# Layer 0's tail in chunks of 8, 4 and 10 tiles, split early tables, and other places for the gather buffers

## The chip, the cores and the metric

The kernel runs on one core of a Trainium2 chip. A core has TensorE (PE), VectorE (DVE), ScalarE (ACT), GpSimd (POOL) and SyncE (SP), each with its own instruction queue, which it works off in order; between queues, semaphores order the work. The metric is the device time of one execution in microseconds (us).

## The reference, cut to what matters

Four graph layers run over N = 2708 nodes with D = 128 features. `adj` is a 2708 x 2708 matrix with about 0.3% of its entries non-zero, each row scaled to sum one.

```python
# layer 0: hyperbolic layer on h = relu(layernorm(x))
h = h_add(h_mul(h, embed), embed_bias)
neigh = exp_map_zero(adj @ log_map_zero(h))
x = x + h_add(h_mul(concat(h0, neigh), layer), layer_bias)   # h0: the layer's input
# layer 1: messages over edges, on h = relu(layernorm(x))
s = h @ msg_w[:, :D].T
d = h @ msg_w[:, D:].T
messages = gelu(s[:, None, :] + d[None, :, :] + msg_b)
aggregated = einsum('ijd,ij->id', messages, adj)
new = concat(h, aggregated) @ upd_w.T + upd_b
x = x + layernorm(gelu(new) + h)
# layer 2: x += relu(adj @ (h @ W));  layer 3: x += h @ W_self + (adj @ h / deg) @ W_neigh
```

In the hyperbolic layer, `exp_map_zero` takes a norm and a tanh, `log_map_zero` a norm and an arctanh (by logarithms), and `h_add` some dot products and a division for every row. Layer 1 needs, for each node i, the rows d[j] of its neighbours j: only those are gathered.

## The kernel before, in words

The nodes lie in T = 22 tiles of 128 rows (the last has 20), and six blocks: five of 4 tiles and one of 2. The dense products with `adj` of layers 0, 2 and 3 are made with a mask (non-zero or not) per block of columns and three bf16 parts of the other operand (`add_product`, 66 matmuls for a block of layer 0). The value by which the mask is scaled is one number per row, `val`, which POOL gathers from `adj`.

From the mask the kernel also finds, for each node, the columns of its neighbours. PE packs the mask into words (`words_in`, `pack`: 22 matmuls and some for the transpose `wp`), VectorE finds up to 24 of them by repeated maxima (`find_words`) and turns them into indices (`find_columns`, `lay_out`). The first 6 neighbours of a node have places of their own: 2 of them (EARLY) are gathered ahead of the loop into `early`, 4 (HEAD − EARLY) in the loop into `g`. All further ones go to the tail: 3 chunks of 128 edges a tile, gathered into `gt` by indices `tail_c`, which `mark_edges` and `pack_edges` prepare. A neighbour beyond the reach of the early table has the index of a row of large negative numbers (`none`) in its early place, and is put in the tail.

Layer 0's tail is what follows each block's product: `neighbours` (norm, tanh, product with half of `layer`, sums of squares), then in `update` `log_factor` and `moebius` (small instructions on one number per row, Ln and Tanh on ScalarE), the new x with its statistics, and `normal_form` (layer 1's layernorm as scale and offset). Then, for each block, `normal_tiles` (relu on ScalarE, transpose hTpm on PE, copy) and the product d on PE, a copy of d into `v` on ScalarE, and a write of d from SP's queue to tables in memory. Before the change all of this runs in two chunks: blocks 0, 1 and 2 (12 tiles), and the late ones 3, 4 and 5 (10 tiles). One table `d_early` holds the d of the first 12 tiles; `d_hbm` holds all. In the middle of the kernel the order is:

```python
        product(2, sums)
        neighbours([0, 1, 2], sums)
        ...
        last = add_product(4, acc, range(split_at))
        formed = update([0, 1, 2], nc.scalar.copy, last)
        ...
        find_columns(slice(groups[3].stop, T))
        gather_early(range(first_half))
        ...
        last = neighbours(late, sums)
```

`find_columns` ends with the gathers of `val` (one per tile) on POOL's queue. `gather_early` puts one gather per tile and early slot on that queue. So POOL's queue holds, one behind the other: val of the last six tiles, 24 early gathers of tiles 0 to 11, 18 of the late tiles, and then those of the loop.

The loop runs over the tiles: for each, `messages` issues 4 gathers into `g` and up to 3 into `gt`, VectorE adds the row's own part, ScalarE takes gelu, and PE sums. Matmuls of layer 2 (`two`) fill PE between tiles. `prelude` prepares a group's own parts on PE, VectorE and ScalarE: that of group 0 runs after all six `pack_edges`, those of later groups in the loop. The gather buffers come from the pool `gath` (4 of each kind), which is opened after the pools of the first part are closed, so that its memory is that of tiles of the first part, and a gather waits until those are done with. `queue_behind` sets an order for the scheduler, which otherwise fills each engine's queue by priority.

After the last tile come the rest of layers 2 and 3.

Of the kernel before, what the change touches and what calls it, by code (L numbers as in the profile page):

```python
# [556 lines left out]
def sparse_stack(  # L557
# [169 lines left out]

    d_hbm = dram.tile([NP + 1, D], F32, name="d_hbm")
    d_early = dram.tile([first_half * P + 1, D], F32, name="d_early")
# [18 lines left out]
    def load_later():  # L748

        nc.gpsimd.dma_start(out=d_hbm[NP : NP + 1, :], in_=none)  # L750
        nc.gpsimd.dma_start(out=d_early[first_half * P :, :], in_=none)
        for w, src in (
            (msg_w, msg_wt),
            (upd_w, upd_wt),
            (w2_w, w2),
            (self_w, w_self),
            (neigh_w, w_neigh),
        ):
            nc.gpsimd.dma_start(out=w, in_=src.rearrange("(a p) o -> p a o", p=P))
        for r, src in ((msg_br, msg_b), (upd_br, upd_b), (ln_wr, ln_w), (ln_br, ln_b)):  # L760
            nc.gpsimd.dma_start(out=r, in_=src.partition_broadcast(P))
# [25 lines left out]


# [7 lines left out]
    with ExitStack() as st:  # L796

        words_p = st.enter_context(tc.tile_pool(name="words", bufs=2))
        left_p = st.enter_context(tc.tile_pool(name="left", bufs=2))
        wide = st.enter_context(tc.tile_pool(name="wide0", bufs=1))  # L800
# [9 lines left out]
        shifts = wide.tile([P, T, P], BF16, name="shifts")  # L810
        for t in range(T):
            nc.gpsimd.tensor_scalar_mul(shifts[:, t, :], ident, float(2 ** (T - 1 - t)))

        spread = r_all[:, full, tails(full) * P :]
        nc.gpsimd.memset(spread, 0.0)
        apart = wide.tile([P, HEAD, rest], F32, name="apart")
# [19 lines left out]
        place = wide.tile([P, P], I32, name="place")  # L836
# [85 lines left out]
        def normal_tiles(sl, name, copy, after=None):  # L922

            n = sl.stop - sl.start
            for t in range(sl.start, sl.stop):
                nc.scalar.activation(  # L926
                    h[:, t, :],
                    x[:, t, :],
                    AF.Relu,
                    bias=node("nb")[:, t : t + 1],  # L930
                    scale=node("rstd")[:, t : t + 1],
                )
# [24 lines left out]
        def times_bias(w, bias, out, name):  # L957
# [3 lines left out]
            wT = pair_p.tile([P, P], F32, tag="wT", name=f"wT{name}")  # L961
# [60 lines left out]
        def pack(b):  # L1022
# [4 lines left out]
            for t in range(T):  # L1027
                nc.tensor.matmul(  # L1028
                    pk[:, :w], shifts[:, t, :], mask[:, t, sl], start=(t == 0), stop=(t == T - 1)
                )  # L1030
            return pk

        def words_in(b):
# [5 lines left out]
            pk = pack(b)  # L1039
# [87 lines left out]

        def lay_out(sl):
# [5 lines left out]
            from_c = float((T - first_half + 1) * P)  # L1134
# [4 lines left out]
            nc.vector.tensor_scalar(near, first[:, :, :EARLY], from_c, None, op0=ALU.is_ge)  # L1139
            nc.vector.scalar_tensor_tensor(  # L1140
                cand[:, sl, 2, SLOTS - EARLY :],
                first[:, :, :EARLY],
                from_c,
# [7 lines left out]
                -(from_c + first_half * P),  # L1151
# [4 lines left out]
            if sl.stop < T:  # L1156
                nc.vector.tensor_scalar_add(early_c[:, sl, :], miss, float(first_half * P))
# [92 lines left out]
        def pack_edges(b, after):  # L1250

            t0, t1 = blocks[b]
            n = t1 - t0
            px = ps_one.tile([P, BANK], F32, tag="one", name=f"ex{b}")
            px = px[:, : n * NQ * 32].rearrange("p (t q c) -> p t q c", t=n, c=32)
            for k in range(n):
                t = t0 + k
                for q in range(NQ):
                    with queue_behind(after):
                        nc.tensor.matmul(  # L1260
                            px[:, k, q, : TAIL + 3],
                            r_all[:, t, q * P : (q + 1) * P],
                            edge_x[:, t, :] if q < tails(t) else short_x,
                            start=True,
                            stop=True,
                        )
            ex = small.tile([P, BLOCK, NQ, TAIL + 3], F32, tag="ex", name=f"exs{b}")
            nc.scalar.copy(ex[:, :n], px[:, :, :, : TAIL + 3])  # L1268
            m = n * NQ
            kth, past, jump = (  # L1270
                small.tile([P, BLOCK * NQ], F32, tag=name, name=f"{name}{b}")[:, :m]
                for name in ("kth", "past", "jump")
            )
            flat_ex = ex.rearrange("p t q c -> p (t q) c")[:, :m, :]
            edge = small.tile([P, BLOCK, NQ], F32, tag="edge", name=f"edge{b}")[:, :n, :]
# [3 lines left out]
                tail_r[:, t0:t1, :].rearrange("p t q -> p (t q)"), flat_ex[:, :, TAIL + 2]  # L1279
            )  # L1280

            nc.vector.tensor_sub(kth, edge, flat_ex[:, :, TAIL])
            nc.vector.tensor_tensor(past, edge, flat_ex[:, :, TAIL + 1], ALU.is_ge)
            nc.vector.tensor_sub(jump, flat_ex[:, :, TAIL], flat_ex[:, :, TAIL + 1])
# [4 lines left out]
            sel = small.tile([P, BLOCK * NQ, TAIL], F32, tag="sel", name=f"sel{b}")[:, :m, :]  # L1289
# [6 lines left out]
            nc.vector.tensor_mul(sel, sel, flat_ex[:, :, :TAIL])  # L1296
            cf = small.tile([P, BLOCK * NQ], F32, tag="cf", name=f"cf{b}")[:, :m]
            nc.vector.tensor_reduce(cf, sel, AX.X, ALU.add)
            nc.vector.tensor_scalar_add(
                tail_c[:, t0:t1, :].rearrange("p t q -> p (t q)"), cf, MID  # L1300
            )
            if t1 == T:
                q = (n - 1) * NQ + tails(full)
                nc.vector.tensor_mul(sel[:, q, :HEAD], is_place, flat_ex[:, q, :HEAD])
                nc.vector.tensor_reduce(cf[:, q : q + 1], sel[:, q, :HEAD], AX.X, ALU.add)
                nc.vector.tensor_scalar_add(
                    tail_c[:, full, tails(full) : tails(full) + 1], cf[:, q : q + 1], MID
                )
# [47 lines left out]
        def neighbours(bs, sums):  # L1356
# [3 lines left out]
            nc.vector.tensor_mul(n_sq, sums[0][:, : sl.stop - sl.start], val[:, sl])  # L1360
            nc.vector.tensor_mul(n_sq, n_sq, val[:, sl])
            _, r, n = norm(n_sq, sl, "k")
            nc.scalar.activation(th, n, AF.Tanh)
# [6 lines left out]
            for t0 in range(sl.start, sl.stop, 3):  # L1370
                g = slice(t0, min(t0 + 3, sl.stop))
                ps = tiles_times(g, yT, layer_w[:, 1, :], f"ne{t0}")
# [19 lines left out]
        def update(bs, copy, after):  # L1392
# [21 lines left out]
            formed = normal_form(sl)  # L1414
            for b in bs:
                g = groups[b]
                n = g.stop - g.start
                normal_tiles(g, f"m{b}", copy, after)
# [3 lines left out]
                for table, end in ((d_early, first_half), (d_hbm, T)):  # L1422
# [7 lines left out]
            return formed  # L1430
# [88 lines left out]
        def gather_early(ts):  # L1519
            for t in ts:  # L1520
                n = rows(t)
                for k in range(EARLY):
                    nc.gpsimd.indirect_dma_start(  # L1523
                        out=early_d[t // EACH][:n, t % EACH, k, :],
                        out_offset=None,
                        in_=d_early,
                        in_offset=bass.IndirectOffsetOnAxis(ap=early_c[:n, t, k : k + 1], axis=0),
                    )
# [3 lines left out]
        sums = sums_of([0, 1, 2])  # L1532
# [10 lines left out]
        end_product(1, acc, sums)  # L1543
        lay_out(halves[0])
        with queue_behind(scaled):
            nc.vector.tensor_scalar(
                spread[:, : HEAD * rest].rearrange("p (k r) -> p k r", r=rest), apart, 0.0, None,
                op0=ALU.is_equal, saturate=False,
# [5 lines left out]
        find_words(3, words_in(3))  # L1554
        find_columns(groups[3])
        read_block(4)
        product(2, sums)
        neighbours([0, 1, 2], sums)
        read_block(5)
        sums = sums_of(late)  # L1560
        product(3, sums)
        words = {b: words_in(b) for b in (4, 5)}
        acc = begin_product(4)
        split_at = BLOCK
        last = add_product(4, acc, range(split_at))
        formed = update([0, 1, 2], nc.scalar.copy, last)
        find_words(4, words[4], formed)
# [5 lines left out]
        add_product(4, acc, range(split_at, T), latest["times"])  # L1573
        end_product(4, acc, sums)
        find_words(5, words[5], formed)
        product(5, sums)
        find_columns(slice(groups[3].stop, T))
        gather_early(range(first_half))
# [5 lines left out]
        with queue_behind(last):  # L1584
            nc.vector.tensor_scalar_add(
                early_c[:, halves[1], :], late_c, float(first_half * P)
            )
        gather_early(range(first_half, full))
        formed = update(late, nc.vector.tensor_copy, None)
        for b in (2, *late):  # L1590
            mark_edges(b, formed)
        for b in range(nb):
            pack_edges(b, latest["times"])
# [98 lines left out]

    group_p = held.enter_context(tc.tile_pool(name="group", bufs=3))
    with ExitStack() as st_m:
        hot_p = st_m.enter_context(tc.tile_pool(name="hot", bufs=3))
        gath_p = st_m.enter_context(tc.tile_pool(name="gath", bufs=4))
        small = st_m.enter_context(tc.tile_pool(name="small1", bufs=2))
        junk_p = st_m.enter_context(tc.tile_pool(name="junk", bufs=1))

        def prelude(g):  # L1700

            sl = groups[g]
            n = sl.stop - sl.start
            for t in range(sl.start, sl.stop, 2):
                two = slice(t, min(t + 2, sl.stop))
                m = two.stop - t
                ps = ps_one.tile([P, BANK], F32, tag="one", name=f"own{t}")
                ps = ps[:, : m * 2 * D].rearrange("p (n j d) -> p n j d", j=2, d=D)
                for k in range(m):
                    nc.tensor.matmul(  # L1710
                        ps[:, k, :, :],
# [347 lines left out]
```

## Time and profile before

| | us |
|---|---|
| median of 3 runs (range) | 554.39 (553.61 to 556.01) |
| the profiled execution's own time | 553.8 |
| its span | 552.0 |
| PE busy | 420.9 (76%) |
| VectorE busy | 422.0 (76%) |
| ScalarE busy | 239.5 (43%) |
| POOL busy | 237.2 (43%) |
| mean granted TensorE clock | 0.892 |

The span is the time from the first to the last instruction that the profiler saw; some 1.8 us of the execution's time lie around it. The page cuts the span into 40 slices of 13.8 us and gives each engine's busy share in tenths; layer 0's tail is in slices 7 to 15. In the timelines a line has start, duration, engine, line of the kernel, operation, output and input, and in brackets how long the engine was idle ahead of it and what ended the wait.

### The profile page before, as it was taken

To read this page: it belongs to the slowest core of one execution; us is meant where nothing else is said; L and a number is where in the kernel's file an instruction comes from. 1 tells how busy PE (TensorE), PEld (TensorE's weight loads), DVE (VectorE), ACT (ScalarE), POOL (GpSimd) and SP (SyncE) were. 2 spreads that over 40 slices of the span, in tenths; PEclk is the share of its full clock that TensorE was granted. 3 is DMA by queue.
4 is the path that set the end of the run, shared out by engine and by line. 5 is a ranking of instruction groups with operands and counts; after the bars stand their busy time and mean duration, and the time that the engine had idled before them with its cause. 6 is when DMAs were issued, how large, how long until landed. Compare 5 with 4: busy or idle time off the path is not lost.

```text
span 552.0 us, 8233 instructions
## 1 busy us (share of the span) xinstructions
PE 420.9 (76%) x2504; PEld 266.1 (48%) x2504; DVE 422.0 (76%) x1743; ACT 239.5 (43%) x570; POOL 237.2 (43%) x268
## 2 busy tenths in 40 slices
PE   1981999999994071376786869859878999989994
PEld 1760344464753051264654656646545455445652
DVE  6877977767998989537788787986656699998742
ACT  2867966766424131324643545444644344300100
POOL 8900022220047777777777777777770000000000
PEclk9995899999997555568897999998998999999998
DMA  8893779970041132123246364672220150399111
GB/s 263 292 300 128 228 243 334 310 212 2 1 116 48 48 92 52 52 52 100 53 153 199 109 195 153 173 232 54 54 52 7 66 237 1 120 382 386 36 57 51
DMA packets 39332, 77.89 MB, mean 141 GB/s; under 512 B 5754, under 2 KB 18614, under 8 KB 37722
## 3 DMA queue, kind: packets, MB, share of 16 engines
q1 hardware_dynamic: 30270, 63.15, 33.1%
q0 software_dynamic: 7264, 13.40, 9.8%
q10 hardware_dynamic: 1744, 0.72, 0.5%
q8 instruction: 22, 0.36, 0.3%
q14 instruction: 32, 0.26, 0.1%
HBM read 73.63 MB, written 3.62 MB: 140 GB/s over the span
## 4 chain that ended last, share of the span: by engine, by line
DVE 34%; PE 32%; issue 9%; POOL 8%; ACT 8%; DMA 7%; ACTq 0%; DVEq 0%; SPq 0%
PE three L1645 8%; PE acc L1324 6%; POOL g L1727 4%; PE two L1645 3%; POOL gt L1727 3%; DVE eq L1661 3%; PE msg L1789 2%; DMA a<-in_adj_t_dram 2%; PE pk L1028 2%; DMA layer_w<-in_L_gnn_layer_dram 2%; DMA g<-d_hbm,head_c 1%; PE u L1458 1%; PE d L948 1%; PE msg L1791 1%; ACT h L1626 1%
## 5 line engine op out<-in xcount | busy, mean ns | idle before, releaser
L1645 PEld LDWEIGHTS <-parts 128*128 128x128 bf16 x792 | 74.5, 99 | 79.8 <-ACT parts L1630 4.4
L1727 POOL DMA_INDIRECT g<-d_hbm,head_c x84 | 83.3, 991 | 25.8 <-issue 20.4
L1645 PE MATMUL two<-mask,parts 128*128 128x512 fp8e4 (+1 forms) x396 | 82.0, 361 | 3.3 <-ACT parts L1630 3.1
L1324 PE MATMUL acc<-mask,parts 128*128 128x512 fp8e4 (+1 forms) x396 | 80.3, 358 | 0.4 <-DVE parts L786 0.4
L1645 PE MATMUL three<-mask,parts 128*128 128x512 fp8e4 (+1 forms) x396 | 79.0, 354 | 0.6 <-ACT parts L1630 0.5
L1727 POOL DMA_INDIRECT gt<-d_hbm,tail_c x65 | 63.1, 971 | 19.8 <-issue 15.5
L1120 POOL DMA_INDIRECT val<-in_adj_dram,ai x22 | 22.1, 1003 | 104.0 <-DVE left L1108 91.2
L1324 PEld LDWEIGHTS <-parts 128*128 128x128 bf16 x396 | 36.9, 98 | 47.1 <-ACT parts L783 7.5
L1523 POOL DMA_INDIRECT early<-d_early,early_c x42 | 43.0, 1023 | 12.8 <-issue 11.6
L1789 PE MATMUL msg<-ident,early 128*128 128x128 f32 x84 | 17.0, 333 | 39.7 <-DVE gt L1778 29.4
L999 ACT ACTIVATE mask<-a 128x2048 fp8e4<-128x2048 uint32 (+3 forms) x27 | 38.2, 1434 | 10.6 <-DMA a<-in_adj_t_dram 10.5
L1661 DVE TENSOR_SCALAR_CACHE_REDUCE eq<-row,val 128x2708 fp8e4<-128x2708 f32 (+1 forms) x13 | 39.4, 3030 | 4.4 <-DMA row<-in_adj_dram 4.3
L1028 PE MATMUL pk<-mask,shifts 128*128 128x512 fp8e4 (+1 forms) x132 | 31.3, 376 | 12.5 <-ACT mask L999 12.5
L1789 PEld LDWEIGHTS msg<-ident,early 128*128 128x128 f32 x84 | 13.2, 222 | 43.5 <-DVE gt L1778 21.9
L1661 DVE TENSOR_SCALAR_CACHE_REDUCE eq<-hT,val 128x1354 fp8e4<-128x1354 f32 x18 | 29.2, 1620 | 0.0
L1789 PE MATMUL msg<-ident,g 128*128 128x128 f32 x168 | 27.8, 318 | 0.0
L1789 PEld LDWEIGHTS msg<-ident,g 128*128 128x128 f32 x168 | 26.1, 233 | 0.3
L1775 DVE TENSOR_TENSOR g<-g,v 128x512 f32<-128x512 f32 x21 | 14.5, 692 | 15.2 <-DMA g<-d_hbm,head_c 15.2
L1710 PE MATMUL own<-pair_w,hT 128*128 128x256 f32 x44 | 15.4, 489 | 13.5 <-ACT exs L1268 9.6
L926 ACT ACTIVATE h<-x,n_nb,n_rstd 128x128 f32<-128x128 f32 x44 | 18.1, 485 | 16.6 <-DVE n_nb L920 16.6
L1791 PE MATMUL msg<-rt,gt 128*128 128x128 f32 x130 | 22.1, 317 | 0.7 <-ACT gt L1784 0.7
L936 PE MATMUL hTpm<-ident,h 128*128 128x128 f32 x22 | 5.6, 350 | 21.7 <-ACT h L926 21.7
(407 smaller groups left out, 877.1 us busy)
## 6 DMA issues: line engine op xcount, KB each, us to landing
a<-in_adj_t_dram SPq DMA_DIRECT2D x25, 1024.0 KB, 7.4
row<-in_adj_dram SPq DMA_DIRECT2D x12, 1354.0 KB, 9.3
hT<-in_adj_dram SPq DMA_DIRECT2D x18, 677.0 KB, 4.1
a<-in_adj_t_dram SPq DMA_DIRECT2D x5, 296.0 KB, 4.6
g<-d_hbm,head_c POOLq DMA_INDIRECT x84, 2.7
a<-in_adj_t_dram SPq DMA_DIRECT2D x5, 256.0 KB
d_hbm<-v SPq DMA_DIRECT2D x5, 256.0 KB, 3.7
out_dram<-x SPq DMA_DIRECT2D x5, 256.0 KB
```

The source lines that it names most:

```text
L926: nc.scalar.activation(h[:, t, :], x[:, t, :], AF.Relu, bias=node("nb")[:, t : t + 1], scale=node("rstd")[:, t : t + 1],)
L999: nc.scalar.activation(mask[:, g : g + n, sl], bits[:, :n, :w], AF.Sign, saturate=False)
L1028: nc.tensor.matmul(pk[:, :w], shifts[:, t, :], mask[:, t, sl], start=(t == 0), stop=(t == T - 1))
L1120: nc.gpsimd.indirect_dma_start(out=val[:, t : t + 1], out_offset=None, in_=flat, in_offset=bass.IndirectOffsetOnAxis(ap=ai[:, t : t + 1], ...
L1324: last = nc.tensor.matmul(acc[:, :w], parts[:, t, k, :], mask[:, t, sl], start=(t == 0 and k == 0), stop=(t == T - 1 and k == 2),)
L1523: nc.gpsimd.indirect_dma_start(out=early_d[t // EACH][:n, t % EACH, k, :], out_offset=None, in_=d_early, in_offset=bass.IndirectOffsetOnAx ...
L1645: last = nc.tensor.matmul(accs[b][:, : sl.stop - sl.start], parts[:, t, k, :], mask[:, t, sl], start=(t == 0 and k == 0), stop=(t == T - 1 ...
L1661: last = nc.vector.tensor_scalar(eq[:n, : c1 - c0], a, val[:n, t : t + 1], None, op0=ALU.is_equal, op1=ALU.add, accum_out=same[:n, t, k : ...
L1710: nc.tensor.matmul(ps[:, k, :, :], hT[:, (t + k) * P : (t + k + 1) * P], pair_w[:, 0::2, :], start=True, stop=True,)
L1727: nc.gpsimd.indirect_dma_start(out=g[:n, q, :], out_offset=None, in_=d_hbm, in_offset=bass.IndirectOffsetOnAxis(ap=table[:n, q : q + 1], a ...
L1789: nc.tensor.matmul(sums, part, ident, start=(q == 0), stop=False)
L1791: done = nc.tensor.matmul(sums, gt[:, q, :], rt[:, q, :], start=(not own_places and q == 0), stop=(q == nq - 1),)
```

## The change

Layer 0's tail is cut in three chunks: blocks 0 and 1 (8 tiles), block 2 (4 tiles), and the late blocks (10 tiles). The early table becomes two: `d_early8` with the first 8 tiles, read by early slot 0, and `d_early12` with the first 12, read by slot 1. The limits in `lay_out` become small tiles with one value per slot. The making of d leaves `update` and is a function of its own, `make_d`, whose parts get places of their own in the queues.

```diff
+    reach = [groups[1].stop, first_half]
-    d_early = dram.tile([first_half * P + 1, D], F32, name="d_early")
+    d_early = [dram.tile([n * P + 1, D], F32, name=f"d_early{n}") for n in reach]
...
-            nc.vector.tensor_scalar(near, first[:, :, :EARLY], from_c, None, op0=ALU.is_ge)
+            nc.vector.tensor_tensor(near, first[:, :, :EARLY], each(from_c, n), ALU.is_ge)
...
-        def update(bs, copy, after):
+        def update(bs):
...
-            formed = normal_form(sl)
+            return normal_form(sl)
+
+        def make_d(bs, copy, after=None, relu_after=None):
             for b in bs:
                 g = groups[b]
-                normal_tiles(g, f"m{b}", copy, after)
+                normal_tiles(g, f"m{b}", copy, after, relu_after)
                 ps = tiles_times(g, hT, msg_w[:, 1, :], f"d{b}", mirrored=True)
                 nc.scalar.copy(d, ps)
-                for table, end in ((d_early, first_half), (d_hbm, T)):
+                for table, end in ((d_early[0], reach[0]), (d_early[1], reach[1]), (d_hbm, T)):
```

The order written out by hand becomes (the middle part of it):

```diff
+        neighbours([0, 1], sums)
+        words = {3: words_in(3)}
+        read_block(4)
+        sums = sums_of([2])
+        product(2, sums)
+        times = times_layer([2])
+        acc = begin_product(3)
+        last = add_product(3, acc, range(2 * BLOCK))
+        read_block(5)
+        words.update((b, words_in(b, last)) for b in (4, 5))
+        last = add_product(3, acc, range(2 * BLOCK, 4 * BLOCK), latest["pack"])
+        formed = update([0, 1])
         lay_out(halves[0])
...
+        done = neighbours([2], sums, formed, times)
+        make_d([0, 1], nc.scalar.copy, last, latest["th"])
+        find_words(3, words[3])
         find_columns(groups[3])
...
+        gather_early(range(first_half), [0])
+        sums = sums_of(late)
+        add_product(3, acc, range(4 * BLOCK, T), last)
+        end_product(3, acc, sums)
+        acc = begin_product(4)
+        last = add_product(4, acc, range(T))
         end_product(4, acc, sums)
+        formed = update([2])
+        find_words(4, words[4], done)
+        find_words(5, words[5], done)
+        make_d([2], nc.scalar.copy, last)
         product(5, sums)
         find_columns(slice(groups[3].stop, T))
-        gather_early(range(first_half))
+        gather_early(range(first_half), [1])
...
-        gather_early(range(first_half, full))
-        formed = update(late, nc.vector.tensor_copy, None)
+        gather_early(range(first_half, full), range(EARLY))
+        formed = update(late)
+        make_d(late, nc.vector.tensor_copy)
```

On POOL's queue the 12 gathers of early slot 0 of tiles 0 to 11 now stand ahead of the six late gathers of val; behind val come the 12 of slot 1, the 18 of the late tiles and the loop. On PE's queue the packs of blocks 4 and 5 and the transposes and products hTpm0, d0, hTpm1, d1 stand inside block 3's product, hTpm2 and d2 inside block 5's. On ScalarE's queue the relus of blocks 0 and 1 stand behind the tanh of block 2's `neighbours`.

`pack_edges` takes one or two blocks at a time, and `prelude` of group 0 is issued after the first of them, with scratch memory of its own:

```diff
-        for b in range(nb):
-            pack_edges(b, latest["times"])
+        through = latest["times"]
+        packed = pack_edges([0], through)
...
+        first = prelude(0, ps_one, lambda t, m: halves_of[t // 2], packed)
+        pack_edges([1, 2], through)
+        pack_edges(late[:2], through)
+        pack_edges(late[2:], through)
...
+    gath_p = held.enter_context(tc.tile_pool(name="gath", bufs=4))
     group_p = held.enter_context(tc.tile_pool(name="group", bufs=3))
...
-        gath_p = st_m.enter_context(tc.tile_pool(name="gath", bufs=4))
```

The pool `gath` is opened ahead of `group`, and so lies over the tiles of the pools `words`, `left` and a new pool `first0` (the shift matrices of the packs and two tables of positions), all of which are used for the last time in the first part.

## The prediction

> **What bounds the kernel now.** I read the table of busy tenths first, then the costliest groups, then the timeline of POOL, and last the timelines of VectorE and ScalarE around the places where POOL stood still.
>
> ```profile
> PE   1981999999994071376786869859878999989994
> PEld 1760344464753051264654656646545455445652
> DVE  6877977767998989537788787986656699998742
> ACT  2867966766424131324643545444644344300100
> POOL 8900022220047777777777777777770000000000
> PEclk9995899999997555568897999998998999999998
> ...
> L1727 POOL DMA_INDIRECT g<-d_hbm,head_c x84 | 83.3, 991 | 25.8 <-issue 20.4
> ...
> L1727 POOL DMA_INDIRECT gt<-d_hbm,tail_c x65 | 63.1, 971 | 19.8 <-issue 15.5
> L1120 POOL DMA_INDIRECT val<-in_adj_dram,ai x22 | 22.1, 1003 | 104.0 <-DVE left L1108 91.2
> ...
> L1523 POOL DMA_INDIRECT early<-d_early,early_c x42 | 43.0, 1023 | 12.8 <-issue 11.6
> ```
>
> POOL is busy only 43% of the span, but its digit is 7 without a break from slice 12 to slice 29, with only "issue" between instructions. A stretch of 7s with no other releaser is an engine that can go no faster: one gather takes about 0.95 us and 0.30 us of issue. The timeline gives the ends of that stretch:
>
> ```profile
> 157.61 0.95 POOL L1120 DMA_INDIRECT val<-in_adj_dram,ai  x1 [38.20 <-DVE left L1108]
> ...
> 164.41 1.34 POOL L1120 DMA_INDIRECT val<-in_adj_dram,ai  x1 [0.30 <-issue]
> 166.05 0.94 POOL L1523 DMA_INDIRECT early<-d_early,early_c  x1 [0.31 <-issue]
> ...
> 222.03 1.03 POOL L1727 DMA_INDIRECT g<-d_hbm,head_c  x1 [0.53 <-ACT parts L783]
> ...
> 412.53 0.95 POOL L1727 DMA_INDIRECT gt<-d_hbm,tail_c  x1 [0.30 <-issue]
> ```
>
> From 157.61 to 413.48 POOL runs 6 + 42 + 84 + 65 = 197 gathers in 255.9 us, 1.30 us each. Before that it idles 38.2 us for column indices from VectorE. After it come 552.0 − 413.5 = 138.5 us in which PE is the dense engine. So the span is (start of POOL's last run) + 255.9 + 138.5, and what the change can move is that start, or a hole inside the run.
>
> The hole is near: the first loop gather needs all of layer 1's d in memory. On VectorE and ScalarE:
>
> ```profile
> 169.66 0.17 DVE L1360 TENSOR_TENSOR n_nsq<-nsq,val 128x10 f32<-128x10 f32 x1 [1.24 <-DMA early<-d_early,early_c]
> ...
> 192.16 0.17 DVE L920 SCALAR_TENSOR_TENSOR n_nb<-n_tn,n_rstd 128x10 f32<-128x10 f32 x1
> ```
> ```profile
> 203.54 0.37 ACT L1421 COPY v<-d 128x256 f32<-128x256 f32 x1 [1.64 <-PE d L948]
> ```
>
> The late ten tiles begin at 169.66, which is 5.25 us after the last val gather was issued at 164.41: the first wait there is for val, whatever releaser is named. The last d copy ends at 203.91, its write is issued at 203.95, and transfers of that size are over by about 206.5 in the DMA view. That is 36.8 us after 169.66. POOL itself reaches the loop at 222.03, so the late chain has 15.5 us to spare now.
>
> [...] a g gather lands 2.7 us after its issue (median), and a 256 KB d write 3.7 us. [...] every gather from a d table is charged the landing of the write, as the chain of waits does. [...] The trace shows the load at 1.28 us and the next activation 0.02 us behind it; I charge 1.28. [...] 0.17 us for 12 columns and 0.17 us for 10. A chunk cut in two pays its small instructions twice.
>
> **The change part by part.**
>
> *Chunks 8 and 4 in place of 12.* VectorE issues a second set of small instructions: some 16 in neighbours, 45 in log_factor and moebius, 15 in normal_form. A dependent one takes 0.20 us from start to start, an interleaved one 0.08. In the trace neighbours took 2.5 us up to n_rk, log and moebius 126.7 to 135.5 less a wait of 2.5, normal_form 2.6. That is 11 to 13 us more VectorE work, of which a part is interleaved with find_words. Two to three table loads more cost ScalarE 1.28 each. In exchange the first 8 tiles need no third block, and three idle spots of VectorE (2.46 at 107.06, 4.60 at 120.00, 2.48 at 129.85) can be filled.
>
> *When the first gather can start.* In the changed order POOL's long run begins with 12 gathers (tiles 0 to 11, first slot) from a table of the first 8 tiles. My hand timeline, from rows of before, on VectorE: find_words(3) from 110.8 (its wt cast now sits behind one more mask), 5.2 us, then n_t at 118.4. ScalarE has three masks (1.91 and 0.70 us) and a table load ahead of n_e: 122.8. Moebius 1.9: 124.7. x and its statistics 2 × 2.9: 130.5. normal_form 2.6: 133.1. neighbours of block 2 runs next and its tanh ends at about 136; the eight relus are queued behind that on ScalarE, with two casts and the squares, until 141.8. PE in its written order (66 matmuls of a block 14.4 us, two packs of 22) is at hTpm0 at 139.6, and at about 143 with a stall of 2.7 us that I count at nsq2, which waits for ScalarE. Then hTpm0, its copy (0.58), d0, the logarithms and n_e in between (1.28 + 0.21 each table), the second copy, d1, v copied at 150.6. The write is issued at 150.7; landing takes 3.4, between the 3.28 of one d write in the chain of waits and the median of 3.7, which gives **154.1**, against 157.61 now: 3.5 us earlier. Bounds: with no ScalarE queueing and no PE stall 147; with the same terms doubled 163.
>
> *The vals behind those 12.* The late column indices are ready at about 156, but the six val gathers now stand behind 12 others: 12 × 1.28 = 15.4 us. Their last is issued at start + 15.4 + 6.8, and the late chain begins 5.25 later, at start + 27.4 = 181.5 instead of 169.66. VectorE would be ready at about 167 and PE at 173 to 174, so both wait for val: here the stall goes. Queued behind that n_nsq on VectorE is the whole late chain, 14 mark_edges and the edge packs. The late d lands 36.8 later, at start + 64.2, or 218.3. This is the cover of the 15.5 us, now used up.
>
> *POOL's own way to the loop* has the same 48 gathers as now, 64.4 us (222.03 − 157.61). It arrives at start + 64.4 too. So both limits meet, and the first g is at about start + 64.5 = 218.6. The gain there is 222.03 − 218.6 = 3.4 us.
>
> *Buffers and packs.* Now the gather buffers lie over tiles that the packs and the prelude last use; after, over tiles done much earlier. That removes the 0.53 us ending in "ACT parts", and more importantly keeps VectorE's later end from holding POOL: the packs, now 45 instructions in place of 68, end at about 230 in the changed order. The first tail indices (about 220) are due to POOL at about 227. I cost this at nothing beyond the above; with the old placement the prelude's end would have been late next.
>
> *Tables and queues.* Two more 256 KB writes on SP, and one more row of 512 B on POOL's queue early on: SP's d writes are 2.2 us apart now, so some 0.4 us of issue each hides, except the one in front of the 8-tile table, already in 154.1. Constants per slot and the different early misses replace like with like: nothing. PE's total work stays the same.
>
> *Loop and end.* In the loop PE's last use of a tile's buffers precedes POOL's reuse by 13 to 21 us (tile 0: 237.3 against 258.05), so a shift of 3 or 4 us passes through to 409.9, and the 138.5 us after it stay.
>
> Sum: the profiled execution is 553.8 us (span 552.0). 553.8 − 3.4 = 550.4. The median of the runs shown is 554.39, 0.6 above it; I say 550.5, since the timeline is no better than that.
>
> **The rivals.** *A larger gain.* For it: PE has no natural wait before 139.6, and VectorE's idle spots hold 9.5 us. If the first gather starts at 148, everything moves until PE's 174 becomes the limit of the late chain: 174 + 36.8 = 210.8 for d, and 212.4 for POOL: about 9.6 us, 544. Against it: five ScalarE waits stand in a row before d1's copy.
>
> *Slower, by one mechanism.* The first d is now on an in-order path: ScalarE's relus behind a tanh that needs VectorE, PE's hTpm0 behind 48 matmuls of block 3 and two packs, the copies behind a table load. And the vals, which need none of that, are queued behind gathers that do. Each us that d1's write lands later costs one us in POOL's run and one in the late chain. The deciding point is a start at 157.6; at 160.4 it is 0.5% slower. A start at 163 gives 163 + 64.5 − 222.03 = 5.5 us, 559. For it: the 13 us of extra small VectorE work and three table loads are certain, the filling of the idle spots is not.
>
> *No change.* The chain ends between 154.8 and 160.4, and early gathers only swap places with vals: 551 to 556.6. That the buffers still hold POOL is not to be seen in the order of instructions; if it were so, the first g would wait for the prelude at about 225, also slower by 3 us.
>
> **How the numbers follow.** 0.5%, about what a measurement of this kernel can tell from no change, is 2.8 us. Start 3 to 6 us earlier: 0.38. Larger gain: 0.10. No change: 0.20. Slower: 0.32, because an in-order path across three engines is seldom as short as its rows. The likeliest case's own range is 548 to 551.6; the range that holds 8 in 10 goes from 544.5 to 560.
>
> **What would show it.** Right: POOL's first early gather at about 154, ahead of all late vals; n_nsq of the late tiles at about 181 with a wait of about 10 us for val; the first g at about 218.6, released by d's write or following without a gap; the last gt ending at about 410; 138.5 us after it. Wrong: a first early gather after 158, or a gap on POOL ahead of the first g of over 3 us, or gaps later in the loop, or an end that is not 138.5 us long.

## The result, and the profile after

The changed kernel takes 550.85 us (median; 548.81 to 553.86), the kernel before, on the same chips, 553.36 us (550.91 to 556.01). The ratio is 0.996, with a 95% interval of 0.9943 to 0.9977: faster by 0.4%. The forecast was 550.5 us, with a gain of 3.4 us; the gain of the medians is 2.5 us. As the next sections show, the sum came out near because two of its terms were wrong by some 4 us each, with opposite signs: that is luck. One run, of 551.61 us in the first experiment, was in a slower state of the chip: it is left out of the ratio there, and the median, 545.45, is 544.22 without it.

The page of the changed kernel, its busy tenths for POOL and its groups of gathers (line, engine, operation, output and input, count, then busy time, mean ns of one, and the idle time ahead with its main releaser):

```profile
POOL 8900022220087777777777777777770000000000
...
L1788 POOL DMA_INDIRECT g<-d_hbm,head_c x84 | 81.5, 971 | 25.6 <-issue 20.1
...
L1788 POOL DMA_INDIRECT gt<-d_hbm,tail_c x65 | 64.9, 999 | 19.8 <-issue 15.8
...
L1580 POOL DMA_INDIRECT early<-d_early,early_c x42 | 47.8, 1138 | 39.8 <-DMA d_early<-v 27.3
...
L1160 POOL DMA_INDIRECT val<-in_adj_dram,ai x22 | 21.0, 954 | 71.0 <-DVE left L1148 56.4
```

POOL's unbroken stretch begins one slice earlier (slice 11 instead of 12, counted from 0; a slice is 13.7 us). The long wait of POOL is now ended by the write of d to an early table, and a mean early gather takes 1138 ns instead of 1023. POOL's timeline shows where that comes from:

```profile
150.17 0.95 POOL L1580 DMA_INDIRECT early<-d_early,early_c  x1 [27.28 <-DMA d_early<-v]
...
157.75 0.99 POOL L1580 DMA_INDIRECT early<-d_early,early_c  x1 [0.30 <-issue]
159.05 5.90 POOL L1580 DMA_INDIRECT early<-d_early,early_c  x1 [0.30 <-issue]
165.26 0.94 POOL L1580 DMA_INDIRECT early<-d_early,early_c  x1 [0.30 <-issue]
...
176.51 0.94 POOL L1160 DMA_INDIRECT val<-in_adj_dram,ai  x1 [0.31 <-issue]
...
218.28 0.94 POOL L1788 DMA_INDIRECT g<-d_hbm,head_c  x1 [0.30 <-ACT exs L1314]
...
408.87 0.94 POOL L1788 DMA_INDIRECT gt<-d_hbm,tail_c  x1 [0.30 <-issue]
```

The run starts at 150.17, 7.44 us earlier than before. But the 48 gathers up to the first g take 68.11 us and not 64.42: one of them, at 159.05, takes 5.90 us. The last gather ends at 409.81. The span is 547.1 instead of 552.0, which adds up as −7.44 (start) + 3.69 (the 48 gathers) + 0.08 (the 149 gathers of the loop, 191.53 against 191.45) − 1.23 (what follows, 137.29 against 138.52) = −4.90. The last of these terms is not counted to the change: over the ten executions profiled here that stretch took 137.3 to 141.2 us. That it was at its shortest in this execution may also be why the execution (548.94 us) lies under its own median.

VectorE during the long gather (start, duration, line, operation):

```profile
158.45 1.13 DVE L1282 SCALAR_TENSOR_TENSOR r_all<-edge_i,n_off,before 128x384 fp8e4<-128x384 f16 x2
...
162.54 0.54 DVE L1279 TENSOR_SCALAR before<-edge_i,n_end 128x384 f16<-128x384 f16 x2
163.00 1.14 DVE L1282 SCALAR_TENSOR_TENSOR r_all<-edge_i,n_off,before 128x384 fp8e4<-128x384 f16 x2
169.09 0.17 DVE L1257 COPY n_off<-po 128x10 f32<-128x10 f32 x1 [4.95 <-PE po L1256]
...
179.63 0.17 DVE L1413 TENSOR_TENSOR n_nsq<-nsq,val 128x10 f32<-128x10 f32 x1 [9.93 <-DMA val<-in_adj_dram,ai]
```

From 157.91 to 164.14 VectorE works off the eight mark_edges of blocks 0 and 1 with no gap. The gather ends at 164.95, 0.81 us after the last of them. The late n_nsq at 179.63 waits 9.93 us for val, and the first g waits for nothing but its turn.

### The profile page after: what moved, and what is told of

Its sections match the earlier page's. It is cut to its first block, busy times and chain, and to the rows that moved or that the text cites. A ratio compares the mean times of both kernels' runs of the same rounds, so it can differ in the third digit from the quotient of the medians.

```text
span 547.1 us, 8301 instructions
## 1 busy us (share of the span) xinstructions
PE 411.4 (75%) x2504; PEld 257.6 (47%) x2504; DVE 424.8 (78%) x1805; ACT 241.8 (44%) x576; POOL 241.1 (44%) x269
## 4 chain that ended last, share of the span: by engine, by line
DVE 33%; PE 24%; POOL 12%; ACT 10%; issue 10%; DMA 10%; ACTq 0%; DVEq 0%; SPq 0%; POOLq 0%
PE three L1727 9%; POOL g L1788 5%; PE two L1727 3%; POOL gt L1788 3%; POOL early L1580 3%; DMA g<-d_hbm,head_c 3%; DMA a<-in_adj_t_dram 3%; PE msg L1850 2%; DVE eq L1743 2%; ACT mask L1034 2%; DMA layer_w<-in_L_gnn_layer_dram 2%; PE acc L1366 1%; DMA gt<-d_hbm,tail_c 1%; PE u L1516 1%; ACT h L1708 1%
## 5 line engine op out<-in xcount | busy, mean ns | idle before, releaser
L1788 POOL DMA_INDIRECT g<-d_hbm,head_c x84 | 81.5, 971 | 25.6 <-issue 20.1
L1727 PE MATMUL two<-mask,parts 128*128 128x512 fp8e4 (+1 forms) x396 | 83.3, 365 | 3.3 <-ACT parts L1712 3.1
L1788 POOL DMA_INDIRECT gt<-d_hbm,tail_c x65 | 64.9, 999 | 19.8 <-issue 15.8
L1580 POOL DMA_INDIRECT early<-d_early,early_c x42 | 47.8, 1138 | 39.8 <-DMA d_early<-v 27.3
L1160 POOL DMA_INDIRECT val<-in_adj_dram,ai x22 | 21.0, 954 | 71.0 <-DVE left L1148 56.4
L1803 PE MATMUL msg<-parts,r_all 128*128 128x128 bf16 x195 | 15.4, 228 | 22.9 <-ACT exs L1314 19.9
L1850 PE MATMUL msg<-ident,g 128*128 128x128 f32 x168 | 26.2, 305 | 0.0
L1803 PEld LDWEIGHTS <-r_all 128*128 128x128 fp8e4 x195 | 12.8, 102 | 25.9 <-issue 20.0
L1850 PEld LDWEIGHTS msg<-ident,g 128*128 128x128 f32 x168 | 24.4, 219 | 0.2
```

The lines of the kernel that those rows point to most:

```text
L1160: nc.gpsimd.indirect_dma_start(out=val[:, t : t + 1], out_offset=None, in_=flat, in_offset=bass.IndirectOffsetOnAxis(ap=ai[:, t : t + 1], ...
L1580: nc.gpsimd.indirect_dma_start(out=early_d[t // EACH][:, t % EACH, k, :], out_offset=None, in_=d_early[k], in_offset=bass.IndirectOffsetOn ...
L1727: last = nc.tensor.matmul(accs[b][:, : sl.stop - sl.start], parts[:, t, k, :], mask[:, t, sl], start=(t == 0 and k == 0), stop=(t == T - 1 ...
L1788: nc.gpsimd.indirect_dma_start(out=g[:n, q, :], out_offset=None, in_=d_hbm, in_offset=bass.IndirectOffsetOnAxis(ap=table[:n, q : q + 1], a ...
L1803: latest["source"] = nc.tensor.matmul(ps[:, q * D : (q + 1) * D], r_all[:, t, q * P : (q + 1) * P], parts[:, t, k, :], start=(k == 0), sto ...
L1850: nc.tensor.matmul(sums, part, ident, start=(q == 0), stop=False)
```

## The experiments

Two theories stood against each other. **Theory 1**: POOL's run sets the end, its start is what the change gained, and the row of marks on VectorE holds a gather of POOL's up, the one of 5.90 us, and takes half of the gain back. **Rivals**: the long gather is chance or comes from the d writes; or the late chain behind val, the chunks or the buffers set the first g.

**Marks while POOL is idle.** The marks of blocks 0 and 1 move to where POOL waits for d, behind n_t of block 2 (`latest["t"]`; the line that keeps it is left out here).

```diff
         formed = update([2])
+        for b in (0, 1):
+            mark_edges(b, latest["t"])
...
-        for b in (0, 1):
-            mark_edges(b, formed)
```

> The changed kernel, with the eight mark_edges of blocks 0 and 1 moved on VectorE's queue from behind lay_out (157.91 to 164.14 in the changed kernel's trace, while POOL issues gathers) to behind n_t of block 2 (about 143.5 to 150, while POOL waits). Theory 1 [...]: no early gather over 2.2 us before the vals, the 48 gathers from the first early one to the first g in 62 to 64 us instead of 68.1, first g at about 213.5, execution 4 to 5 us shorter than that of the changed kernel with the 5.9 us gather, so about 544 to 547. Rival (the long gather comes from the d writes or from chance on the DMA side): a gather of 3 us or more is still there or is there in some runs, time as the changed kernel's, 549 to 551. Second rival (late d is the limit just behind): POOL gains but stops ahead of the first g for the d_hbm write; first g no earlier than about 215.5.

It took 545.45 us, 0.9864 of the kernel before (0.9828 to 0.9901). POOL's timeline of this run:

```profile
148.38 1.56 POOL L1580 DMA_INDIRECT early<-d_early,early_c  x1 [27.28 <-DMA d_early<-v]
...
170.34 0.94 POOL L1160 DMA_INDIRECT val<-in_adj_dram,ai  x1 [0.30 <-issue]
...
200.21 2.07 POOL L1580 DMA_INDIRECT early<-d_early,early_c  x1 [0.30 <-issue]
...
212.19 0.94 POOL L1788 DMA_INDIRECT g<-d_hbm,head_c  x1 [0.30 <-ACT exs L1314]
```

No gather before the vals takes over 1.56 us, and the 48 gathers take 63.81 us (212.19 − 148.38), 4.3 less than in the changed kernel. That the run also starts 1.8 us earlier is no more than what its start differs by between kernels with the same order ahead of it (147.96 to 150.17). Two of the eight tiles' marks were still left over when POOL began; they ran between other instructions and held no gather. The first g still has no wait of its own. Theory 1 holds, the rival of the d writes does not: they are still there, at the same place.

**Marks twice.** The suspected cost is doubled, in time that VectorE had idle.

```diff
         for b in (0, 1):
             mark_edges(b, formed)
+        for b in (0, 1):
+            mark_edges(b, formed)
```

> The changed kernel, with the eight mark_edges of blocks 0 and 1 issued twice at their place (same values written again, VectorE's row of marks 12.4 us long instead of 6.2; VectorE was idle after it until 179.6). Theory 1 (the row of marks starves POOL): the stretched gathers inside the row add up to about 10 to 12 us instead of 5.0 over their usual length, first g about 6 us later (224), time 555 to 557. Rival (the 5.9 us gather has another cause): VectorE's idle time hides the second row, the time stays at 549 to 552.

It took 557.56 us, 1.0071 of before (1.0036 to 1.0106), 6.7 more than the changed kernel. POOL, and the last marks of the row on VectorE:

```profile
158.93 11.97 POOL L1580 DMA_INDIRECT early<-d_early,early_c  x1 [0.30 <-issue]
```
```profile
168.94 1.14 DVE L1282 SCALAR_TENSOR_TENSOR r_all<-edge_i,n_off,before 128x384 fp8e4<-128x384 f16 x2
```

One gather took 11.97 us, ending at 170.90, again 0.82 after the row's end at 170.08. The first g was at 223.95.

**Vals first.** The `gather_early` of slot 0 is issued behind `find_columns` of the late tiles.

```diff
-        gather_early(range(first_half), [0])
         ...
         find_columns(slice(groups[3].stop, T))
+        gather_early(range(first_half), [0])
```

> The changed kernel, with the six late val gathers put ahead of the twelve slot-0 early gathers on POOL's queue. The prediction's account (POOL's run is the limit, and the late chain behind val has as much room): POOL's run starts when the late column indices are ready, about 153.2 instead of 150.2; the late tiles' n_nsq moves from 179.6 to about 172, where PE ends; the end moves later by the 3 us of the start, to 552 to 554. Rival (the late chain behind val sets the first g): the first g comes earlier, and the time falls by 2 us or more, to 547 to 549.

It took 550.4 us (0.9951, 0.993 to 0.9971), like the changed kernel, and not the 552 to 554 expected. The edit did less than described: the scheduler left four of the twelve early gathers ahead of the vals, so POOL began at 149.22 and not later. But the question is answered. The late n_nsq came at 169.11, 10.5 us earlier than in the changed kernel, and the first g at 217.50, no earlier than POOL's own pace allows (68.28 us after the start, with a val gather of 5.91 us beside the marks). An earlier late chain brought nothing; in this kernel it costs nothing that the vals stand behind others.

**Gather buffers at the old place.**

```diff
-    gath_p = held.enter_context(tc.tile_pool(name="gath", bufs=4))
...
         hot_p = st_m.enter_context(tc.tile_pool(name="hot", bufs=3))
+        gath_p = st_m.enter_context(tc.tile_pool(name="gath", bufs=4))
```

> The changed kernel, with the pool gath opened where it was before the change, behind group and hot, so that the gather buffers lie over other tiles of the first part. The prediction's account (with the old place the end of the packs or of the prelude would hold the first loop gathers): POOL stands still ahead of some g or gt until VectorE's packs are done (tail_c of the last block at 241.8 in the changed kernel's trace, prelude at 221), 3 to 20 us, time 552 to 570. Rival (the place of the buffers does not matter, since POOL has no slack to lose there): no wait of POOL over 1 us ahead of g, 549 to 552.

It took 563.35 us, 1.019 of before (1.0143 to 1.0236). The first g on POOL:

```profile
231.44 0.94 POOL L1788 DMA_INDIRECT g<-d_hbm,head_c  x1 [15.96 <-DVE tail_c L1348]
```

POOL stood still for 15.96 us until tail_c, the end of the last pack on VectorE (230.61). With the packs and the prelude in their new order, the new place of the buffers is what keeps VectorE out of POOL's way.

**One early table.** Both slots read the table of 12 tiles; all early gathers stand behind val, as before (the line that names the tables is left out here).

```diff
-    reach = [groups[1].stop, first_half]
+    reach = [first_half, first_half]
...
-        gather_early(range(first_half), [0])
...
+        gather_early(range(first_half), [0])
         gather_early(range(first_half), [1])
```

> The changed kernel with the early tables not split: both slots read a table of the first 12 tiles, and all 24 early gathers of tiles 0 to 11 stand behind the six late vals on POOL's queue, as before the change; chunks, PE and ScalarE order, packs and buffers stay as changed. The prediction's account (the gain is POOL's earlier start, which only the 8-tile table gives): POOL issues val from about 153 to 160, then waits for block 2's d, which lands at about 170 (its write is issued at 166.4 in the changed kernel's trace), then needs 42 gathers of 1.27 us, so the first g is at about 223 to 224, that is 5 to 6 us later than in the changed kernel; 555 to 557. Rival (the gain comes from the chunks themselves or from the buffers): first g at about 218 and 549 to 552.

It took 556.9 us, 1.0078 of before (1.0053 to 1.0103). POOL's timeline:

```profile
151.89 1.10 POOL L1160 DMA_INDIRECT val<-in_adj_dram,ai  x1 [30.19 <-DVE left L1148]
...
158.57 1.34 POOL L1160 DMA_INDIRECT val<-in_adj_dram,ai  x1 [0.30 <-issue]
168.41 0.94 POOL L1580 DMA_INDIRECT early<-d_early,early_c  x1 [8.50 <-ACT v L1385]
...
223.58 0.94 POOL L1788 DMA_INDIRECT g<-d_hbm,head_c  x1 [0.30 <-issue]
```

The vals are done at 159.9, POOL waits 8.50 us, and the first g is at 223.58, as worked out. The releaser named in the bracket is an instruction that ended near by; what the gather needs is block 2's d. Without the small table the rest of the change makes the kernel slower than it was.

**Marks broken up.** The marks stay beside the gathers, but behind each second mark instruction stands one with a single input: a bn_stats, which takes the statistics of a tile of x.

```diff
-                nc.vector.scalar_tensor_tensor(r_all[:, t, :w], ...)
+                mark = nc.vector.scalar_tensor_tensor(r_all[:, t, :w], ...)
+                if b < 2:
+                    with queue_behind(mark):
+                        nc.vector.bn_stats(bst[:, t, :], x[:, t, :])
```

> The changed kernel, with one bn_stats of a tile of x (one input, results not used again) behind each of the eight second mark instructions of blocks 0 and 1, at their old place beside POOL's gathers; VectorE has 1.8 us more to do, in time in which it was idle. Theory 1a ([...] a single-input instruction between them lets it in): no gather before the vals over 2.5 us, the twelve gathers and six vals lose at most 2 us together, time 546 to 548.5. Theory 1b (the fp16 mark instructions hold POOL off as well, or any row without idle time does): a gather of 6 us or more, ending about 0.8 us after the end of the row at about 166, time 551 to 553.

It took 546.43 us, 0.9887 of before (0.9846 to 0.9929). VectorE, and POOL at the same time:

```profile
158.14 0.53 DVE L1279 TENSOR_SCALAR before<-edge_i,n_end 128x384 f16<-128x384 f16 x2
158.58 0.60 DVE L1282 SCALAR_TENSOR_TENSOR r_all<-edge_i,n_off,before 128x384 fp8e4<-128x384 f16 x1
159.11 0.28 DVE L1293 BATCH_NORM_STATS2 hst<-x 128x6 f32<-128x128 f32 x1
159.32 0.59 DVE L1282 SCALAR_TENSOR_TENSOR r_all<-edge_i,n_off,before 128x384 fp8e4<-128x384 f16 x1
```
```profile
157.28 0.94 POOL L1583 DMA_INDIRECT early<-d_early,early_c  x1 [0.30 <-issue]
158.53 0.95 POOL L1583 DMA_INDIRECT early<-d_early,early_c  x1 [0.30 <-issue]
159.78 0.95 POOL L1583 DMA_INDIRECT early<-d_early,early_c  x1 [0.30 <-issue]
```

VectorE has as little idle time between the instructions as before, and more to do, yet no gather there takes over 1.02 us, where one took 5.90 in the changed kernel. So the second half of theory 1b fails, that any row without idle time holds POOL off: here it was not VectorE's load that mattered but the kind of instruction. Its first half, that the fp16 mark instructions (`before`, one input) hold POOL off as well as those with two inputs (`r_all`, from edge_i and before), is not decided, since the bn_stats breaks up their rows too. But a row of instructions with two inputs held a gather without them: in the kernel before, x is made with rows of fp32 instructions with two inputs, and a gather of 2.10 us stands beside one. POOL's gather, and the last of the row beside it:

```profile
186.06 2.10 POOL L1523 DMA_INDIRECT early<-d_early,early_c  x1 [0.30 <-issue]
```
```profile
186.22 1.13 DVE L1408 SCALAR_TENSOR_TENSOR x<-layer_b,n_cb,x 128x128 f32<-128x128 f32 x4
```

The row ends at 187.35 and the gather at 188.16, 0.81 later, while VectorE goes on with bn_stats. The first gather of the first experiment, the one of 1.56 us, is another: it ends 0.83 after such a row (149.11).

The runs show which instructions held the gathers and for how long: POOL was held to the end of the row of marks, 5 and 11 us beyond the usual 0.94 us of a gather, and not for one instruction, which takes 0.30 to 0.61 us there. By what means VectorE holds POOL was not shown. Whether the fp16 mark instructions alone, the ones with one input, would hold POOL off too was not tried.

**Marks of block 2 moved as well.** The edit is shown against the first experiment's kernel.

```diff
-        for b in (0, 1):
+        for b in (0, 1, 2):
             mark_edges(b, latest["t"])
```

> As e1_marks_early, with the four marks of block 2 moved as well, so that twelve stand behind n_t and VectorE has 3 us less to do after the late x. Theory 1 (each mark taken out of POOL's busy time gives POOL time back): the late gathers of 1.1 to 2.1 us become fewer, some 1 us is gained on e1_marks_early, 543.5 to 545.5. Rival (the marks now reach beyond 148, where POOL's run begins, and hold up its first gathers and the x of block 2): a gather of 3 us or more near 150, time 545.5 to 549.

It took 544.66 us, 0.9848 of before (0.9815 to 0.9882), not to be told from 545.45. The 48 gathers took 63.39 us: three late gathers take over 1.15 us instead of five, but a first gather of 1.58 us beside the x of block 2 remains, as in the first experiment.

**Both remedies.** As the first experiment, and the fourteen other tiles' marks broken up with bn_stats.

> As e1_marks_early (marks of blocks 0 and 1 behind n_t), and with one bn_stats, results not used again, behind each second mark instruction of the fourteen other tiles, which VectorE works off beside the late early gathers; VectorE has 2.8 us more to do there. Theory 1 (single-input instructions let POOL in): the gathers of 2.07, 1.26 and 1.17 us in e1_marks_early's late marks go to at most 1.05; the 1.85 beside the late x stays; POOL reaches the first g about 1.5 us earlier relative to its start (62.3 instead of 63.8 us); time 543.5 to 545. Rival (the longer marks hold up the copies of the late d, whose landing becomes the limit): POOL waits ahead of the first g for the d_hbm write, 545 to 547.

It took 545.12 us, 0.9873 of before (0.9837 to 0.9908). POOL ahead of the loop:

```profile
209.06 1.35 POOL L1583 DMA_INDIRECT early<-d_early,early_c  x1 [0.30 <-issue]
211.90 1.12 POOL L1791 DMA_INDIRECT g<-d_hbm,head_c  x1 [1.50 <-DMA d_hbm<-v]
```

The 2.07 us gather is gone, though two of 1.36 and 1.35 us beside the marks are left, where at most 1.05 was expected. But now POOL waits 1.50 us for the write of the late d. The rival's mechanism took over, and the gain of theory 1 went into it: this is the next limit. In the first experiment it had been about 1.8 us away: the last copy of d ended 1.45 us earlier there, so that its write would have been in place at about 210.4, against 212.19 for POOL.

## Why the prediction was right, and where it was not

- **What bounds the kernel** was right: POOL's run passes any shift of the first g on. From the first g to the end of the last gather it took 190.8 to 192.7 us in every run above, whenever it began.
- **The start of the run** was the first mis-sized term. 154.1 was predicted, 150.17 measured (147.96 to 150.17 in the runs with the same order ahead of it). In the timelines PE stood still for 0.26 us at nsq2 where I charged 2.7, hTpm0 ran at 140.31 and not 143, and n_e came at 120.27 and not 122.8. From hTpm0 to the end of v's copy it took 6.4 us instead of 7.6. These two, 2.7 and 1.2 us, are the whole difference. The landing was right: 3.4 charged, 3.47 from the write's issue at 146.70.
- **POOL's way to the loop** was the second: "the same 48 gathers as now, 64.4 us". The duration was taken from another neighbourhood on VectorE. Before the change the eight marks lay partly among find_columns and beside val gathers, which they stretched by 0.9 us together; after it they lie in one row, and cost 5.0 us. That VectorE can slow POOL without a wait that the profile shows was missing from the working. The 5.90 and 11.97 us gathers, both with 0.30 us of issue ahead of them, show it, and so does their absence in the first and sixth experiment, where no gather before the vals took over 1.56 and 1.02 us.
- **The vals behind twelve others**: n_nsq was predicted at 181.5 with a wait of about 10 us, and found at 179.63 with 9.93. The agreement is luck: the last val was issued 26.3 us after the start instead of 22.2, because of the stuck gather, and n_nsq followed 3.1 us after it instead of 5.25. The 5.25 rests on a misreading of the kernel before. There the wait ahead of n_nsq was put down to val, but the last nsq product, which n_nsq also reads, ended on PE at 169.63 (168.13 + 1.50, a modelled end), 0.03 us ahead of n_nsq:

```profile
168.13 1.50 PE L1347 MATMUL nsq<-ones_col,hT 128*128 128x1 f32 x12
```

  In the third and fifth experiments n_nsq follows the last nsq by 0.04 us in the same way, and in the fifth the profile names PE:

```profile
168.87 0.17 DVE L1413 TENSOR_TENSOR n_nsq<-nsq,val 128x10 f32<-128x10 f32 x1 [0.35 <-PE nsq L1389]
```

  So the late chain most likely waited for PE before the change. Where it did wait for val, n_nsq came 3.1 us after the last val was issued, in the first experiment too (3.13).
- **"So both limits meet"** was nearly right. POOL came to the first g without waiting for d, and the third experiment shows that 10 us more room there gives nothing. But the room was small: the last copy of d ended at 212.43, and with the 4.2 us from such a copy to the first g in the last experiment POOL could have begun at about 216.6 (an estimate), against 218.28. The stuck gather had held up both, as the vals stood behind it.
- **Buffers and packs, "at nothing beyond the above"**: right, and the reason given, that the old place would have let VectorE's packs hold POOL, is measured by the fourth experiment: 15.96 us of waiting and 12.5 us of time. The packs ended at 242.1 in the changed kernel, and not at about 230, but POOL waited for none of them. The rival on this had the wrong size: it let the first g wait for the prelude at about 225, but it waited for the packs until 231.4.
- **The rivals**: of the larger gain's 9.6 us, 7.4 were there at the start of the run, and POOL's longer way to the loop took half of them back. The slower case did not come about, since its condition, a first d after 157.6, did not. Its price, one us of time for each us by which the first g is late, is roughly borne out by the fourth and fifth experiments: first g 13.2 and 5.3 us later than in the changed kernel, 12.5 and 6.05 us more time.

By the bound stated in the prediction, 0.5%, the measured 0.4% falls into "within 0.5%", to which it gave 0.20, and just misses "faster" with 0.48; the interval leaves no doubt about the sign.

## What to carry to other kernels

When one engine runs without a gap for half of the span, look for its start, and then at the length of each of its instructions: a single stretched one among forty costs as much as a wait (here 5.90 us instead of 0.94), and shows in no list of waits. Where GpSimd's gathers are the limit, try to put VectorE's rows of instructions with two inputs where GpSimd has nothing to issue, or an instruction with one input between them: here that gave 545.45 and 546.43 us instead of 550.85. When a wait has several conditions, look up when each was met, and not only the releaser that is named. A duration carried over from a profile held only beside the same neighbours: the same 48 gathers took 64.42 us before the change and 68.11 after it.

## What was not expected of the hardware

A gather that GpSimd issues was held for as long as VectorE had two-input and fp16 mark instructions back to back: 5.90, 11.97, 5.91 and 5.90 us in four runs, ending 0.81 to 0.82 us after the row in each. One bn_stats of 0.28 us behind each second mark instruction was enough to avoid the long gather (1.02 us at most in the sixth experiment). Not every gather beside such a row is caught. In the kernel before, gathers beside six marks in a row took 1.16 and 1.34 us, and pairs of mark instructions took longer than the 0.54 us they take elsewhere, so there it seems to be VectorE that waited:

```profile
163.73 0.67 DVE L1237 TENSOR_SCALAR before<-edge_i,n_end 128x384 f16<-128x384 f16 x2
```

Beside the first row of x there (182.24 to 184.48) two gathers took 0.94 and 0.95 us. What decides which of the two waits, and whether one does, is open.
